# Two expert results per token kept in a lower and a higher half, read back in two steps, in a one-core Macaron block

## The chip, the core and the metric

The kernel runs on one core of a Trainium2 chip, in one launch. The metric is device time in microseconds (us). A core has these engines: PE (TensorE, matmuls, with PEld for its weight loads), DVE (VectorE), ACT (ScalarE), POOL (GpSimd) and SP (SyncE, which here only issues DMAs). Each engine runs its own instructions in the order in which they were issued, and waits on semaphores for the others. Plain DMAs are issued from SP. Indirect DMAs, which scatter or gather rows by a list of row numbers, are issued from POOL.

## The reference

Eight sequences of 512 tokens, 128 features each, pass through three residual steps:

```python
x = x + 0.5 * ffn(layernorm(x))
x = x + attention(layernorm(x))      # 16 heads of 8, causal
x = x + 0.5 * ffn(layernorm(x))      # the same weights
```

The feed-forward step is a mixture of eight experts, each 128 to 512 to 128 with a ReLU between. A router gives eight logits for a token. The two largest are taken, a softmax over the two gives the gates, and the output is the gated sum of two experts' results:

```python
topk_scores, topk_idx = jax.lax.top_k(logits, 2)
gates = jax.nn.softmax(topk_scores)
out = gates[0] * expert[topk_idx[0]](x) + gates[1] * expert[topk_idx[1]](x)
```

## The kernel before

**Groups.** Each feed-forward step handles the sequences in three groups: f0, f1, f2 for the first, g0, g1, g2 for the second, of 2, 3 and 3 sequences. For each sequence `route` (L801) computes the layernorm, the logits, the ranks and the position of each token in its expert's room. It then scatters every token twice from POOL, once for each of its two experts, to a buffer `xs` in HBM: 4 tiles of 128 tokens times 2 ranks make eight scatters for a sequence (L875). When a group's sequences are all scattered, `experts` (L924) fetches each expert's rows from `xs` into the tile `xb` with one DMA from SP (`fetch`, L933), turns them with PE (`xbT_ps`, L976), copies them into `xT` (L980), multiplies (`z`, L989), applies the ReLU into `h` (ACT at L996, DVE at L998) and multiplies again (`y`, L1013). DVE adds the bias into the tile `ysb` (L1017), and the result goes to a buffer `ys` in HBM.

**Two ways back.** For f0 to g0 each token gathers its two results by row number (`combine`, L1064; POOL gathers at L474; DVE adds at L1073). g1 and g2 are *tagged*: a scattered token carries two more numbers, its row number for rank 0 and its place in the group, so that the expert's side can work out where the token lives (`homes`, L939) and can scatter the result there directly (`send`, L956, four for each expert, L957). In the kernel before, the place is twice the token's number plus the rank, so a token's two results lie side by side. `collect` (L1099) then needs no gather: plain DMAs from SP read `ys` into a tile `yr` (L1110), DVE adds each of the two results, times its gate, to `x` (L1114), and SP writes `x` to the output (L1120). For g2, the last group, all of `collect` follows the last expert's sends: six reads, 24 adds (3 sequences, 4 tiles, 2 results) and six writes.

**Order.** The order on PE, ACT, DVE and SP is written out by hand. The program walks through units. Units 0 to 95 are one step of attention each (8 sequences, 4 head groups, 3 steps); units below 0 come before the attention, and units from 96 to 126 after it. `surround` (L1427) issues one unit: attention, a share (quota) of the current group's expert pieces, and whatever `due` names for this unit. POOL's transfers wait in two lists: `jobs` (the scatters of `route`, the gathers of `combine`) and `results` (the sends). `transfer` (L650) issues the next one of these, and jobs come first. It is called at the start and at the end of a unit, and from unit 96 on also in the middle if more than two are waiting. `transfer(second=True)` takes a job only if one of the waiting jobs is urgent, or if there are more than four and no results. `behind_mark` (L635) makes each transfer also wait for the *mark*: the ReLU, bias addition or attention mask that was issued last before it.

The eighth sequence (number 7) is routed in units 99 to 102, and its scatters are the last ones that g2's first fetch waits for:

```python
routed(u + seq + (3 if b == B - 1 else 4), *place[False][b], urgent=b in (1, 4, 5, 6, 7), ahead=b in (4, 6, 7))
...
combined(79 + 7 * i, g0, i, out)
```

The end of the kernel before is this:

```python
run(fills["g2"][0])
...
while m.results:
    m.transfer()
last = [m.collect(g2, i, out, parts=2) for i in range(3)]
step(*last)
run(*last)
```

Of the kernel before, what the change touches and what calls it, by code (L numbers as in the profile page):

```python
# [11 lines left out]
FP = mybir.dt.float32  # L12
# [436 lines left out]
class Group:  # L449


    def __init__(self, seqs, cap, key, xs, ys, tagged):
        self.seqs, self.cap, self.key, self.xs, self.ys = seqs, cap, key, xs, ys
        self.tagged, self.width = tagged, D + 2 * tagged
        self.ct = -(-cap // P)
        self.rows = cap // self.ct
        assert self.ct * self.rows == cap
        self.parts = [(t, min(3 if cap > 4 * P else 4, self.ct - t))
                      for t in range(0, self.ct, 3 if cap > 4 * P else 4)]
        self.placed = 0  # L460
        self.pieces = E * (len(self.parts) * (1 + C) + self.ct) + 1


# [19 lines left out]
class Main:  # L483
    def __init__(self, tc, ctx, aps):
# [52 lines left out]
        for e in range(4):  # L537
# [4 lines left out]
            if e == 2:  # L542
# [48 lines left out]
                       allow_small_or_imprecise_dtypes=True)  # L591

        self.place = const.tile([P, T], FP, name="place")
        nc.gpsimd.iota(self.place, [[2 * P, T]], base=0, channel_multiplier=2,
                       allow_small_or_imprecise_dtypes=True)

        self.row = {}
# [203 lines left out]
    def route(self, g, i, urgent=False, ahead=False, early=False):  # L801
# [60 lines left out]
        for r in range(2):  # L862
            nc.vector.scalar_tensor_tensor(
                sm[:, :, r, :], rank, float(r), posb, ALU.is_equal, ALU.mult
            )
        nc.vector.tensor_reduce(g.to[:, i], sm, AX.X, ALU.max)
        nc.vector.tensor_scalar(g.back[:, i], g.to[:, i], E * g.cap - 1, None, ALU.min)
        if g.tagged:
            nc.vector.tensor_copy(xn[:, :, D], g.to[:, i, :, 0])
            nc.vector.tensor_scalar(  # L870
                xn[:, :, D + 1], self.place, float(2 * N * i), None, ALU.add
            )

        def scatter(t, r):
            ins = nc.gpsimd.indirect_dma_start(  # L875
# [35 lines left out]
        nc.vector.tensor_scalar(tot, e2, 1.0, 2.0, ALU.add, ALU.mult)  # L911
        nc.vector.reciprocal(g.gates[:, i, :, 0], tot)
        nc.vector.tensor_tensor(g.gates[:, i, :, 1], g.gates[:, i, :, 0], e2, ALU.mult)
        yield

    def close_group(self, g, k):
# [7 lines left out]
    def experts(self, g):  # L924
# [14 lines left out]
        def homes(e, xb):  # L939

            row = self.row[g.cap][:rows]
            second = self.small.tile([P, CT], FP, tag="second", name=f"second_{key}_{e}")
            nc.vector.scalar_tensor_tensor(
                second[:rows, : g.ct], xb[:rows, : g.ct, D], -float(e), row,
                ALU.add, ALU.not_equal,
            )
            nc.vector.tensor_tensor(
                second[:rows, : g.ct], second[:rows, : g.ct], xb[:rows, : g.ct, D + 1], ALU.add
            )
            home[e] = self.small.tile([P, CT], I32, tag="home", bufs=7, name=f"home_{key}_{e}")  # L950
            nc.vector.scalar_tensor_tensor(
                home[e][:rows, : g.ct], row, float(2 * N * len(g.seqs) + e),
                second[:rows, : g.ct], ALU.add, ALU.min,
            )

        def send(e, t, ys):  # L956
            ins = nc.gpsimd.indirect_dma_start(  # L957
                out=g.ys[:, :],
                out_offset=bass.IndirectOffsetOnAxis(ap=home[e][:rows, t : t + 1], axis=0),
                in_=ys[:rows, t, :], in_offset=None,  # L960
            ).ins
            tc.declare_no_dep(ins, group=f"ys_{key}", reason="no two rows have the same home")
            tc.add_to_no_dep_group(f"ys_{key}", ins)
            self.in_turn(ins, scatter=True)
            self.behind_mark(ins)

# [72 lines left out]
        for e in range(E):  # L1039
            if e + 1 < E:  # L1040
                h_next, turns, wides_next = up(e + 1, loaded.pop(0))
            else:
                turns = []

            rest = downs[:1] + turns + downs[1:]
            last = turns[-1] if turns else None
            for i, piece in enumerate(wides):
                piece()
                yield
                k = -(-len(rest) // (len(wides) - i)) if rest else 0  # L1050
                for other in rest[:k]:
                    other()
                    if other is last and e + 3 < E:
                        loaded.append(fetch(e + 3))
                    yield
                rest = rest[k:]
            downs = down(e, h)
            if e + 1 < E:
                h, wides = h_next, wides_next
        for piece in downs:  # L1060
            piece()
            yield
# [36 lines left out]
    def collect(self, g, i, dst, parts=1):  # L1099

        nc = self.nc
        b = g.seqs[i]
        x = self.x[b]
        if i % 2 == 0:
            self.pair = self.p2.tile([P, 2, T, 2, D], FP, tag="ee", name=f"yr_{b}")
        yr = self.pair[:, i % 2]
        src = g.ys[2 * N * i : 2 * N * (i + 1), :].rearrange("(t p r) d -> p t r d", p=P, r=2)
        n = T // parts
        for k in range(parts):
            nc.sync.dma_start(yr[:, ts(k, n)], src[:, ts(k, n)])  # L1110
        yield
        for t in range(T):
            for r in range(2):
                nc.vector.scalar_tensor_tensor(  # L1114
                    x[:, t, :], yr[:, t, r], g.gates[:, i, t, r : r + 1], x[:, t, :],
                    ALU.mult, ALU.add,
                )
            if t % n == n - 1:
                k = t // n
                nc.sync.dma_start(  # L1120
                    dst[b].rearrange("(t p) d -> p t d", p=P)[:, ts(k, n)], x[:, ts(k, n)]
                )
            if parts == 1:
                yield
# [179 lines left out]
def macaron_kernel(  # L1304
# [51 lines left out]
    with ExitStack() as main:  # L1356
# [8 lines left out]
        g0 = m.open_group([0, 1], 351, 1, "g0")  # L1365
        g1 = m.open_group([2, 3, 4], 480, 3, "g1")
        g2 = m.open_group([5, 6, 7], 480, 4, "g2")
        order = [f0, f1, f2, g0, g1, g2]
        place = {True: {}, False: {}}
        for g in order:  # L1370
# [56 lines left out]
        def surround(n, att):  # L1427

            m.unit = n
            now = None  # L1430
            for g, fetch, start, end in plan:
                if n == fetch:
                    close(g)
                    fills[g.key] = [opened(g), g.pieces]
                if n == end:
                    run(fills[g.key][0])
                if start <= n < end:
                    now, until = fills[g.key], end
                    if g is g1 and att:
                        until = end + 7  # L1440
            quota = min(now[1], -(-now[1] // (until - n))) if now else 0
            fill = now[0] if now else iter(())
            if now:
                now[1] -= quota
            if att:
                ee = m.scores(*units[n])
            last, m.oT = m.oT, None
            if m.held is not None:
                got = m.values(*m.held)
                if got is not None:  # L1450
                    m.oT = (*m.held[:2], got)
            m.held = (*units[n], ee) if att else None
            m.evac = "dve" if att and n % seq not in (8, 9, 10) else "act"
            run(take(fill, 1 if quota else 0))
            m.evac = "act"
            if att:
                m.causal(units[n][2], ee, 0)
            m.transfer()
            if last is not None:
                m.outputs(*last)  # L1460
            if att:
                m.causal(units[n][2], ee, 1)
            if not att:
                m.additions()
            work = due.pop(n, [])
            todo = max(quota - 1, 0)
            for k, (stream, steps) in enumerate(work):
                some = todo // (len(work) - k + 1)
                run(take(stream, steps))
                run(take(fill, some))  # L1470
                todo -= some
            if n >= core and len(m.jobs) + len(m.results) > 2:
                run(take(fill, todo // 2))
                todo -= todo // 2
                m.transfer(second=True)
            run(take(fill, todo))
            m.additions()
            m.transfer(second=True)

        m.held = m.oT = None  # L1480
        with m.banks(("m", 8)):
# [32 lines left out]
                at(u + seq + 2, m.finish(b), 2, 2 if b == B - 1 else 1)  # L1514
                routed(u + seq + (3 if b == B - 1 else 4), *place[False][b], urgent=b in (1, 4, 5, 6, 7), ahead=b in (4, 6, 7))
            for i in range(2):
                combined(79 + 7 * i, g0, i, out)
            for i in range(3):
                at(tail + 2 + 3 * i, m.collect(g1, i, out), 5)
            at(tail, m.verdict(bad), 2)  # L1520
# [12 lines left out]
        with m.banks(("m", 8)):  # L1533
            for u in range(core + 2, ends):
                surround(u, False)
            run(fills["g2"][0])
            assert not due, due
            assert not m.jobs and not m.adds
            while m.results:
                m.transfer()  # L1540
            last = [m.collect(g2, i, out, parts=2) for i in range(3)]
            step(*last)
            run(*last)

    flag = nc.values_load(
        bad[0:1, 0:1], min_val=0, max_val=1,
# [50 lines left out]
```

## Time and profile before

| | |
|---|---|
| time, median of 6 runs | 715.13 us (714.58 to 716.67) |
| the profiled execution: own time | 717.68 us |
| its span, first to last instruction | 715.9 us |
| PE busy | 635.2 us (89% of the span) |
| DVE busy | 411.4 us (57%) |
| ACT busy | 340.6 us (48%) |
| POOL busy | 301.0 us (42%) |
| granted TensorE clock, mean | 0.969 |

A view of the timeline shows start, duration, engine, line, operation, output and inputs of an instruction, and in brackets how long the engine was idle before it and what ended that. Instructions that follow each other are merged (x24). The chain of waits goes back from the last instruction, at each step to what released it. SPq and POOLq are the queues' own instructions, such as the issue of a DMA. A DMA's landing is the last update of its semaphore. All times inside the trace are counted from the start of the span.

### The profile page before, as it was taken

What the parts mean: (1) busy time and instruction counts of PE and PEld (TensorE: products, weight loads), DVE (VectorE), ACT (ScalarE), POOL (GpSimd) and SP (SyncE); (2) the same over time, 40 slices, a digit from 0 to 9 for tenths busy, and PEclk for the clock granted to TensorE, in tenths of its full rate; (3) what the DMA queues carried; (4) which work ended last, traced back from release to release, by engine and by line L of the source; (5) the groups of instructions that cost most, each with busy time, mean ns of one, the idle gap of its engine ahead of it and who ended that gap; (6) DMA issues with size and microseconds to landing.
All of it is one profiled execution on the core that took longest, in us unless ns stands there. A gap on an engine that the chain in (4) does not pass through costs nothing.

```text
span 715.9 us, 13045 instructions
## 1 busy us (share of the span) xinstructions
PE 635.2 (89%) x4867; PEld 412.4 (58%) x4867; DVE 411.4 (57%) x1442; ACT 340.6 (48%) x548; POOL 301.0 (42%) x322
## 2 busy tenths in 40 slices
PE   3269989989999999999999999999999988869980
PEld 2158857756556556556656656555555556637760
DVE  6636427735466666675677677676665654233414
ACT  4034433445655665565565565556646532224420
POOL 3744627653122223314153324333244565666560
PEclk9999989999999999999999999999999998969995
DMA  8747733222409931111211110112302111235324
GB/s 263 188 132 223 181 104 97 71 59 73 97 23 152 230 113 40 29 29 35 76 33 45 44 40 30 33 39 60 71 27 73 35 37 33 74 93 136 98 56 140
DMA packets 78670, 61.06 MB, mean 85 GB/s; under 512 B 7392, under 2 KB 70792, under 8 KB 78600
## 3 DMA queue, kind: packets, MB, share of 16 engines
q1 hardware_dynamic: 69608, 42.51, 23.4%
q0 software_dynamic: 8704, 17.63, 8.6%
q8 instruction: 41, 0.67, 0.4%
q14 instruction: 29, 0.24, 0.1%
q10 hardware_dynamic: 288, 0.01, 0.0%
HBM read 26.34 MB, written 33.78 MB: 84 GB/s over the span
## 4 chain that ended last, share of the span: by engine, by line
PE 81%; DVE 5%; DMA 2%; another core or an unknown queue 2%; ACT 2%; issue 1%; POOL 1%; POOLq 0%; ACTq 0%; DVEq 0%
PE st L1201 13%; PE o L1227 11%; PE y_f L1013 11%; PE z_g L989 11%; PE z_f L989 10%; PE y_g L1013 10%; PE qkv_ps_a L1139 3%; PE kT_ps L1178 2%; PE qT_ps L1178 2%; PE otok_ps L1245 2%; PE xbT_ps_f L976 2%; PE xbT_ps_g L976 1%; DVE x L1114 1%; PE proj_ps L1266 1%
## 5 line engine op out<-in xcount | busy, mean ns | idle before, releaser
L1208 ACT ACTIVATE ee<-st 128x768 f32<-128x768 f32 (+1 forms) x192 | 159.0, 881 | 109.6 <-PE st L1201 91.8
L474 POOL DMA_INDIRECT yt_f<-ys,back_f x64 | 64.9, 1014 | 136.7 <-DVE ee L1215 56.0
L1215 DVE TENSOR_TENSOR ee<-ee,keep 128x256 f32<-128x256 f32 (+1 forms) x192 | 93.7, 508 | 26.1 <-ACT ee L1208 26.0
L1013 PEld LDWEIGHTS y_g<-w_sb,h_g 128*120 128x120 f32 (+1 forms) x704 | 87.3, 184 | 27.9 <-issue 22.4
L875 POOL DMA_INDIRECT xs<-xn_g,to_g x64 | 64.0, 1001 | 92.8 <-DVE ee L1215 36.1
L1013 PEld LDWEIGHTS y_f<-w_sb,h_f 128*120 128x120 f32 (+1 forms) x704 | 85.8, 182 | 28.5 <-issue 17.3
L989 PE MATMUL z_g<-xT_g,w_sb 128*128 128x480 f32 (+1 forms) x192 | 94.5, 580 | 8.4 <-ACT xT_g L980 6.0
L1201 PE MATMUL st<-qT,kT 32*128 32x512 f32 (+3 forms) x1024 | 96.1, 467 | 4.0 <-ACT kT L1184 1.7
L1013 PE MATMUL y_f<-w_sb,h_f 128*120 128x128 f32 (+1 forms) x704 | 93.9, 277 | 0.2 <-DVE h_f L998 0.2
L1013 PE MATMUL y_g<-w_sb,h_g 128*120 128x128 f32 (+1 forms) x704 | 93.0, 277 | 0.6 <-DVE o_tok L1250 0.3
L989 PE MATMUL z_f<-xT_f,w_sb 128*128 128x480 f32 (+1 forms) x192 | 91.8, 568 | 1.0 <-ACT xT_f L980 1.0
L1227 PE MATMUL o<-ee,vpad 128*32 128x512 f32 (+3 forms) x1024 | 89.4, 442 | 0.8 <-DVE ee L1215 0.8
L996 ACT ACTIVATE h_f<-z_f,b1T 128x480 f32<-128x480 f32 (+1 forms) x86 | 53.5, 623 | 73.5 <-PE z_f L989 55.9
L957 POOL DMA_INDIRECT ys<-ysb_g,home_g x64 | 64.0, 1000 | 45.6 <-issue 12.1
L1017 DVE TENSOR_TENSOR ysb_f<-y_f,b_sb 120x128 f32<-120x128 f32 (+1 forms) x88 | 25.1, 288 | 82.9 <-PE y_f L1013 65.8
L1017 DVE TENSOR_TENSOR ysb_g<-y_g,b_sb 120x128 f32<-120x128 f32 (+1 forms) x88 | 25.3, 288 | 76.3 <-PE y_g L1013 52.2
L996 ACT ACTIVATE h_g<-z_g,b1T 128x480 f32<-128x480 f32 (+1 forms) x71 | 45.7, 646 | 48.9 <-PE z_g L989 37.9
L1201 PEld LDWEIGHTS st<-qT,kT 32*128 32x128 f32 x1024 | 43.1, 183 | 34.3 <-issue 8.8
L875 POOL DMA_INDIRECT xs<-xn_n,to_f x40 | 39.0, 974 | 37.3 <-issue 8.8
L1227 PEld LDWEIGHTS o<-ee,vpad 128*32 128x32 f32 x1024 | 23.5, 108 | 52.4 <-issue 8.6
L989 PEld LDWEIGHTS z_g<-xT_g,w_sb 128*128 128x128 f32 x192 | 30.7, 198 | 34.7 <-issue 19.7
L989 PEld LDWEIGHTS z_f<-xT_f,w_sb 128*128 128x128 f32 x192 | 31.5, 201 | 14.9 <-issue 9.5
(186 smaller groups left out, 780.8 us busy)
## 6 DMA issues: line engine op xcount, KB each, us to landing
w_sb<-in_L_ffn_W_dram SPq DMA_DIRECT2D x16, 256.0 KB
xs<-zeros SPq DMA_DIRECT2D x8, 487.5 KB
xb_g<-xs SPq DMA_DIRECT2D x16, 243.8 KB
xb_f<-xs SPq DMA_DIRECT2D x16, 240.0 KB
ys<-ysb_f SPq DMA_DIRECT2D x16, 240.0 KB
ys<-zeros SPq DMA_DIRECT2D x2, 1536.0 KB
x<-in_L_attn_x_dram SPq DMA_DIRECT2D x8, 256.0 KB
xs<-zeros SPq DMA_DIRECT2D x1, 1920.0 KB
```

What stands on the lines that cost most here:

```text
L474: ins = op(*args, **kw)
L875: ins = nc.gpsimd.indirect_dma_start(out=g.xs[:, :], out_offset=bass.IndirectOffsetOnAxis(ap=g.to[:, i, t, r : r + 1], axis=0), in_=xn[:, ...
L957: ins = nc.gpsimd.indirect_dma_start(out=g.ys[:, :], out_offset=bass.IndirectOffsetOnAxis(ap=home[e][:rows, t : t + 1], axis=0), in_=ys[:r ...
L989: nc.tensor.matmul(z[:, :n], self.w1_sb[:, e, ts(c, P)], xT[:, n0 : n0 + n], start=True, stop=True,)
L996: ins = nc.scalar.activation(dst, z[:, :n], AF.Relu, bias=bias)
L1013: nc.tensor.matmul(y[:rows], h[:, c, ts(t, rows)], self.w2_sb[:, e, c, :], start=(c == 0), stop=(c == C - 1),)
L1017: ins = nc.vector.tensor_tensor(ys[:rows, t, :], y[:rows], self.b2_sb[:rows, e], ALU.add)
L1178: self.nc.tensor.transpose(tp[:, ts(t, P)], pad[:, t, 4 * g : 4 * g + 4, :].rearrange("p h s -> p (h s)"), self.ident,)
L1201: nc.tensor.matmul(st[:, h, c0 : c0 + N - kt * P], kT[r0 : r0 + SLOT, ts(kt, P)], qT[r0 : r0 + SLOT, kt * P :], start=True, stop=True,)
L1208: nc.scalar.activation(ee[:, two, :width], st[:, two, :width], AF.Exp)
L1215: ins = self.nc.vector.tensor_tensor(d, d, self.keep.unsqueeze(1).unsqueeze(1).to_broadcast([P, 2, len(parts), P]), ALU.min,)
L1227: self.nc.tensor.matmul(self.o[h * SLOT : (h + 1) * SLOT, kt * P :], self.vpads[b % 2][:, kt, 4 * g + h, :], ee[:, h, c0 : c0 + n], start= ...
```

## The change

**Results in two halves.** The first half of `ys` takes, for every token of the group, the result of the one of its two experts that has the lower number, and the second half that of the other one. To tell which is which, `route` compares the expert numbers of the two ranks (`which`, `swap`), puts the lower expert's row number into the tag (`apart`), and swaps the two gates where needed. `homes` now adds N times the number of sequences where a row is not the lower one's. `collect` reads each half with a DMA of its own, [128 x 4 x 128], where a read before took both results, [128 x 4 x 256] for g1 and two of [128 x 2 x 256] for each sequence of g2.

**g2's collect in two steps.** The last expert, number 7, is never the lower of two. The three `collect` streams of g2 are created at the start (`g2.ends`). When the pieces of expert 6 and the upward multiplications of expert 7 have been issued, `experts` first issues all waiting sends and then the reads of the three lower halves. After that come the downward multiplications of expert 7 with its sends, the reads of the higher halves, the 12 adds of the lower results, and the 12 adds of the higher ones with the six writes. A group named "lower" takes out the dependency between the early reads and expert 7's sends.

**Eight scatters in one row.** From unit 98 on two more transfers are issued in the middle of a unit if more than one job is waiting. The eight scatters of sequence 7 are then issued in two units (4 and 4), where they took three (2, 3 and 3).

**Gathers of g0's second sequence** are entered at unit 84, where it was 86.

```diff
-        nc.gpsimd.iota(self.place, [[2 * P, T]], base=0, channel_multiplier=2,
+        nc.gpsimd.iota(self.place, [[P, T]], base=0, channel_multiplier=1,
...
         nc.vector.tensor_reduce(g.to[:, i], sm, AX.X, ALU.max)
+        if g.tagged:
+            which = small.tile([P, T, 2], I32, tag="which", name=f"which_{key}")
+            nc.vector.tensor_scalar(which, g.to[:, i], E - 1, None, ALU.bitwise_and)
+            swap = small.tile([P, T], FP, tag="swap", name=f"swap_{key}")
+            nc.vector.tensor_tensor(swap, which[:, :, 0], which[:, :, 1], ALU.is_gt)
+            apart = small.tile([P, T], FP, tag="apart", name=f"apart_{key}")
+            nc.vector.tensor_tensor(apart, g.to[:, i, :, 1], g.to[:, i, :, 0], ALU.subtract)
+            nc.vector.tensor_tensor(apart, apart, swap, ALU.mult)
+            nc.vector.tensor_tensor(xn[:, :, D], apart, g.to[:, i, :, 0], ALU.add)
+            nc.vector.tensor_scalar(xn[:, :, D + 1], self.place, float(N * i), None, ALU.add)
         nc.vector.tensor_scalar(g.back[:, i], g.to[:, i], E * g.cap - 1, None, ALU.min)
-        if g.tagged:
-            nc.vector.tensor_copy(xn[:, :, D], g.to[:, i, :, 0])
-            nc.vector.tensor_scalar(
-                xn[:, :, D + 1], self.place, float(2 * N * i), None, ALU.add
-            )
...
         nc.vector.tensor_tensor(g.gates[:, i, :, 1], g.gates[:, i, :, 0], e2, ALU.mult)
+        if g.tagged:
+            lo, hi = g.gates[:, i, :, 0], g.gates[:, i, :, 1]
+            nc.vector.tensor_tensor(tot, hi, lo, ALU.subtract)
+            nc.vector.tensor_tensor(tot, tot, swap, ALU.mult)
+            nc.vector.tensor_tensor(lo, lo, tot, ALU.add)
+            nc.vector.tensor_tensor(hi, hi, tot, ALU.subtract)
...
-            nc.vector.tensor_tensor(
-                second[:rows, : g.ct], second[:rows, : g.ct], xb[:rows, : g.ct, D + 1], ALU.add
+            nc.vector.scalar_tensor_tensor(
+                second[:rows, : g.ct], second[:rows, : g.ct], float(N * len(g.seqs)),
+                xb[:rows, : g.ct, D + 1], ALU.mult, ALU.add,
             )
...
+            if e == E - 1 and g.ends:
+                tc.declare_no_dep(ins, group="lower", reason="the last expert is none's lower")
...
             downs = down(e, h)
             if e + 1 < E:
                 h, wides = h_next, wides_next
+        if g.ends:
+
+            while self.results:
+                self.transfer()
+            for collect in g.ends:
+                next(collect)
         for piece in downs:
...
-        src = g.ys[2 * N * i : 2 * N * (i + 1), :].rearrange("(t p r) d -> p t r d", p=P, r=2)
         n = T // parts
-        for k in range(parts):
-            nc.sync.dma_start(yr[:, ts(k, n)], src[:, ts(k, n)])
-        yield
-        for t in range(T):
-            for r in range(2):
-                nc.vector.scalar_tensor_tensor(
-                    x[:, t, :], yr[:, t, r], g.gates[:, i, t, r : r + 1], x[:, t, :],
-                    ALU.mult, ALU.add,
-                )
+        src = g.ys[: 2 * N * len(g.seqs), :].rearrange(
+            "(r b t p) d -> r b p t d", r=2, b=len(g.seqs), p=P
+        )
...
+        ins = nc.sync.dma_start(yr[:, 0], src[0, i])
+        if g.ends:
+            self.tc.add_to_no_dep_group("lower", ins.ins)
+            yield
+        nc.sync.dma_start(yr[:, 1], src[1, i])
+        yield
+        if g.ends:
+            for t in range(T):
+                add(t, 0)
+            yield
+        for t in range(T):
+            if not g.ends:
+                add(t, 0)
+            add(t, 1)
...
                 m.transfer(second=True)
+                if n >= core + 2 and len(m.jobs) > 1:
+                    m.transfer(second=True)
+                    m.transfer(second=True)
...
-                combined(79 + 7 * i, g0, i, out)
+                combined(79 + 5 * i, g0, i, out)
...
-            last = [m.collect(g2, i, out, parts=2) for i in range(3)]
-            step(*last)
-            run(*last)
+            step(*g2.ends)
+            step(*g2.ends)
+            run(*g2.ends)
```

More of the change, by code (lines that the diff above doesn't have):

```diff
@@ L459, in __init__ @@
                       for t in range(0, self.ct, 3 if cap > 4 * P else 4)]
-        self.placed = 0
+        self.placed, self.ends = 0, ()
         self.pieces = E * (len(self.parts) * (1 + C) + self.ct) + 1
@@ L1104, in collect, with add @@
         if i % 2 == 0:
-            self.pair = self.p2.tile([P, 2, T, 2, D], FP, tag="ee", name=f"yr_{b}")
+            self.pair = self.p2.tile([P, 2, 2, T, D], FP, tag="ee", name=f"yr_{b}")
         yr = self.pair[:, i % 2]
-        src = g.ys[2 * N * i : 2 * N * (i + 1), :].rearrange("(t p r) d -> p t r d", p=P, r=2)
         n = T // parts
-        for k in range(parts):
-            nc.sync.dma_start(yr[:, ts(k, n)], src[:, ts(k, n)])
+        src = g.ys[: 2 * N * len(g.seqs), :].rearrange(
+            "(r b t p) d -> r b p t d", r=2, b=len(g.seqs), p=P
+        )
+        def add(t, r):
+            nc.vector.scalar_tensor_tensor(
+                x[:, t, :], yr[:, r, t], g.gates[:, i, t, r : r + 1], x[:, t, :],
+                ALU.mult, ALU.add,
+            )
+        ins = nc.sync.dma_start(yr[:, 0], src[0, i])
[3 more added lines that the diff above has]
+        nc.sync.dma_start(yr[:, 1], src[1, i])
         yield
+        if g.ends:
+            for t in range(T):
+                add(t, 0)
+            yield
         for t in range(T):
-            for r in range(2):
-                nc.vector.scalar_tensor_tensor(
-                    x[:, t, :], yr[:, t, r], g.gates[:, i, t, r : r + 1], x[:, t, :],
-                    ALU.mult, ALU.add,
-                )
+            if not g.ends:
+                add(t, 0)
+            add(t, 1)
             if t % n == n - 1:
@@ L1367, in macaron_kernel @@
         g2 = m.open_group([5, 6, 7], 480, 4, "g2")
+        g2.ends = [m.collect(g2, i, out, parts=2) for i in range(3)]
         order = [f0, f1, f2, g0, g1, g2]
```

## The prediction

> **What bounds the kernel now.** I read the page's busy line first, then its forty slices, because the share of an engine is an average over stages with different limits.
>
> ```profile
> PE 635.2 (89%) x4867; PEld 412.4 (58%) x4867; DVE 411.4 (57%) x1442; ACT 340.6 (48%) x548; POOL 301.0 (42%) x322
> PE   3269989989999999999999999999999988869980
> ```
>
> PE carries the span but for three places: the start, a dip near slice 36, and the last slices. The change touches the second and the third. Next, the busy time by windows (columns: window, length, then busy of PE, PEld, DVE, ACT, POOL, granted clock, DMA share, GB/s), and who PE waits for in the attention stage (us in total, times, longest).
>
> ```profile
> 240.00:590.00 350.00, 341.62 (x2933) 205.38 (x2932) 234.76 (x758) 200.19 (x318) 126.77 (x125) 1.00 0.20 54
> 624.00:634.00 10.00, 1.03 (x4) 0.69 (x4) 0.69 (x4) 0.38 (x1) 5.92 (x6) 0.64 0.62 144
> PE qkv_ps_a L1139 <- DVE o_tok L1250: 1.7, 5, 0.7
> PE o L1227 <- DVE ee L1215: 0.8, 1, 0.8
> ```
>
> In attention PE is busy 341.6 of 350 us; DVE has 115 us to spare, and all PE waits on it add up to 3.2 us. From 624 to 634 PE does almost nothing. The POOL timeline there (start, length, idle time before and its releaser) shows the row of scatters of sequence 7 that g2's first fetch waits for:
>
> ```profile
> 611.48 0.99 POOL L875 DMA_INDIRECT xs<-xn_g,to_g  x1 [1.69 <-DVE ex_g L907]
> 612.77 0.98 POOL L875 DMA_INDIRECT xs<-xn_g,to_g  x1 [0.30 <-issue]
> 615.08 0.96 POOL L875 DMA_INDIRECT xs<-xn_g,to_g  x1 [1.33 <-issue]
> ...
> 621.43 0.97 POOL L875 DMA_INDIRECT xs<-xn_g,to_g  x1 [0.30 <-issue]
> ```
>
> The last lands 2.2 us later, SP issues the fetches at 623.79, the first lands at 627.04. Then the waits of 615 to 640 show something else:
>
> ```profile
> ACT xT_g L980 <- remote: 14.5, 1, 14.5
> ```
>
> ACT takes PE's first transpose only at 633.62, 6 us after it was done by PE's records, so g2's start need not follow the row. What the profile cannot name ("remote") I do not count on.
>
> Last, the chain of waits and the timeline of the tail:
>
> ```profile
> 697.77 2.73 DMA ys<-ysb_g,home_g
> 700.51 0.02 issue
> 700.52 3.01 DMA yr<-ys
> 703.53 0.03 issue
> 703.56 0.36 DVE x L1114
> ...
> 703.56 7.89 DVE L1114 SCALAR_TENSOR_TENSOR x<-yr,gates_g,x 128x128 f32<-128x128 f32 x24 [7.70 <-DMA yr<-ys]
> 704.97 6.87 SPq L1120 DMA_DIRECT2D out_dram<-x  x6
> ```
>
> PE ended at 694.6. The last send leaves at 697.77 and lands 2.73 later; six reads follow, the first landing after 3.01; 24 adds run back to back for 7.89 us; the last write is issued at 711.47 and lands at 713.51. Every one of these is on the path. The sends are paced by POOL, 1.29 us apart, and DVE waited 7.70 us ahead of its adds.
>
> The profiled execution took 717.68 us (span 715.9, and 1.8 around it), 2.55 above the median of 715.13. I work out differences in it and apply them to the median.
>
> **Part 1, the lower half read early: −3.94 us, of which part is given back.** By the order of instructions in the changed kernel, the three lower reads wait for the last send of expert 6, and the three upper reads for the last of expert 7; both stand on SP's queue in that order, with nothing else behind them that is needed earlier. Expert 6's last send was issued at 692.52 and landed at 695.66. So the lower reads leave at about 695.7, the first lands 3.0 us later at 698.7, and the twelve lower adds (12 × 0.329 = 3.95 us) end at about 702.7 if their data keep up, which is ahead of the first upper landing at 703.5. Twelve adds remain behind it: 12 × 0.329 = 3.95 in place of 7.89. The upper reads are three of 256 KB; the six of before landed at 703.53, 704.23, 705.74, 706.40, 707.74 and 708.48, so three come about 1.0 apart, under the 1.31 us that four adds of a sequence take. DVE stays the bound, and the last write goes out 3.94 us sooner. Two writes come per 1.3 us instead of per 2.6; each moves 128 KB, and the writes of before were spread over 6.5 us with the last landing 2.0 after its issue; I add nothing for that and 0.3 in the range. Removed reads cost nothing: total bytes are equal. A read row is now 512 B where two results of a token stood together as 1024 B. In the trace a 1024 B packet takes 54.8 ns on its engine, one of 520 B 34 to 38 and one of 512 B 27 to 31, so half the row is about half the time; at worst (38 against 27.4) the upper reads take 1.4 times their part, 1.4 us per sequence and 0.2 behind the adds, put at 0.5 in the bound.
>
> **What the early reads cost: +0.7 us, from 0 to +2.0.** They run beside expert 7's last scatters. The trace has no read beside a send at the tail, but it has the fetches of g2 (four of 244 KB, issued 623.79 to 625.72) beside g1's sends: those issued at 624.00, 625.30, 626.60 and 627.89 landed 4.70, 4.82, 4.10 and 2.82 us later, and one alone takes 2.73. The last scatter at 697.77 comes 2.1 us after the first early read, as the send at 625.30 to 626.60 does after the fetches; that says +1.4 to +2.1, of which I take 2.0 as the end. But the early reads are three, not four, in fewer bytes (768 KB against 975 KB), and the read queue should be nearly empty (six reads took 8 us, so three take some 5: to 700.5), as for the send at 627.89, which lost 0.1. I take a value between, nearer the later row: +0.7. This is the least certain term of the sum.
>
> [...]
>
> **Part 2, sequence 7's scatters in one row: +0.1 us, from −0.41 to +0.62.** Their transfers move up on the list only, and the order of POOL's instructions is that of before. What changes is the time. On DVE, four more small operations (`which`, `swap`, `apart` twice) stand ahead of the copy of a y piece that the first scatter also waits for (610.91 to 611.20, then +0.28). Small dependent operations follow one another by 0.21 us in the rows of the routing, independent ones by 0.08: 3 × 0.21 + 0.08 = 0.71 us, of which DVE had 0.1 idle. So the first scatter goes at about 612.1, +0.62. Against it stands the gap of 1.33 ahead of the third scatter, where 0.30 is usual and nothing named is waited for: if it is gone in the new order of issue, 1.03 comes back, −0.41 in all. PE's start of g2 need not follow, by the 6 us above. I take +0.1.
>
> **Part 3, DVE's added work in attention: +0.2 us, from 0 to 7.2.** Each tagged sequence gets the 0.71 above and four operations on the gates, another 0.71; five of the six sequences fall beside attention: 5 × 1.43 = 7.2 us on DVE. Its cover is the 115 us in which DVE is idle in that window. The waits of PE on DVE are 3.2 us for 234.8 us of DVE work; in that proportion 7.2 more gives 0.1, and since a routing chain comes in one piece I take 0.2. If the cover were gone, all 7.2 would be PE's.
>
> **What costs nothing.** The first gathers of the second sequence of g0 come two units sooner in the list, but POOL's order does not change by it. Collecting g1 takes six reads instead of three: three more issues of about 0.47 us on SP, whose queue there holds the fetches of `xb` with four buffers, asked for a unit ahead. `homes` has one operation in place of one. If that cover failed, a read ahead of a fetch would cost its 0.47.
>
> **Sum:** −3.94 + 0.7 + 0.1 + 0.2 = −2.94, so 715.13 − 2.94 = 712.2 us.
>
> **The rivals.**
>
> *The row pays and the reads collide with nothing.* −3.94 + 0 − 0.41 = −4.35, so 710.8. For it: the 0.1 of the send at 627.89, and an unexplained gap that may be of one execution. Against it: the three sends before that.
>
> *The early reads hold up expert 7's sends.* The last scatter lands at +2.0 and the upper reads, short rows, lag +0.5; −3.94 + 2.5 + 0.3 (parts 2 and 3) = −1.14, so 714.0: nearly no change. For it: 4.70 and 4.82 against 2.73.
>
> *DVE becomes the bound (the slower side).* A routing chain is serial on DVE between `ee` products (L1215, 508 ns each, 192 of them) that PE's `o` waits for. If every added 1.43 us pushes those products back and PE's buffers are empty by then, PE loses 7.2 us in attention: −2.94 − 0.2 + 7.2 = +4.1, 719.2. It decides from about 3.1 + 1.4 = 4.5 us carried over, 63% of the 7.2. For it: `o <- ee` with 0.8 in one piece. Against it: only 3.2 us of waits of this kind in 350.
>
> *It does not do what it says.* If the lower reads, on one queue with others or for a dependence of the whole buffer `ys`, land only with the upper, all 24 adds stay behind: 0 + 0.1 + 0.2, about 715.4. The order of instructions speaks against it.
>
> **How the numbers follow.** The forecast gets 0.64, with its own range of 711.0 to 713.6 (part 1's collision from 0 to +2.0, the others about their values). The row that pays gets 0.12, the hold-up 0.14, DVE as the bound 0.06, no early read 0.04. The range over all leaves out DVE's case, and the outer ends of those on both sides: 710.4 to 714.8. What a measurement of this kernel can tell from no change is about 0.2%, 1.43 us: below 713.70 is faster, above 716.56 slower. Faster holds the forecast and the row that pays: 0.76. Same holds the hold-up and no early read: 0.18. Slower holds DVE's case: 0.06.
>
> **What would show it.** In the changed profile's tail: three reads issued at about 695.7 less or plus the shift of the stages before, three at about 700.5 to 702; the twelve lower adds done before the first upper read lands; a run of twelve adds of 3.95 us behind it; the last send's landing at 2.7 (no hold-up) to 4.7 us (full hold-up) after its issue. In the middle: the first scatter of sequence 7 at about 612.1, the last at 621.0 to 622.1, and whether ACT's first `xT_g` follows it. In attention: PE busy again about 341 of 350 with PE's waits on DVE near 3 us. I am wrong if PE's waits on DVE grow by over 4 us, if the last lower add ends after the upper reads have landed, or if g2's first matmul moves by over a microsecond.

## The result, and the profile after

The changed kernel takes 722.40 us (median of 17 runs, 717.22 to 725.70) against 715.91 for the kernel before over 38 runs: ratio 1.0082 [1.0063, 1.0102], 6.5 us slower. The profiled execution took 718.07 us (span 716.3), the low end of its runs; its granted clock did not drop around 94 us, where the profile of before has 6.8 us at 0.5. So the two profiles are compared stage by stage.

The busy line and the PE slices of the changed kernel:

```profile
PE 631.6 (88%) x4867; PEld 410.4 (57%) x4867; DVE 416.9 (58%) x1490; ACT 340.0 (47%) x548; POOL 301.5 (42%) x322
PE   3279989999999999999999999989999978649990
```

DVE has 48 more instructions; the dip near slice 36 has grown deeper. The windows and PE's waits in attention:

```profile
240.00:590.00 350.00, 339.85 (x2922) 204.26 (x2919) 236.96 (x790) 200.14 (x315) 127.97 (x125) 1.00 0.18 51
624.00:634.00 10.00, 1.03 (x4) 0.69 (x4) 4.07 (x12) 0.00 (x0) 7.56 (x9) 0.50 0.54 129
PE qkv_ps_a L1173 <- DVE o_tok L1284: 1.7, 5, 0.7
PE o L1261 <- DVE ee L1249: 0.8, 1, 0.8
```

PE's named waits on DVE are those of before. From 624 to 634 POOL is busy 7.56 us, where it was 5.92. Its timeline from sequence 7's scatters on (POOL), ACT's wait from 615 to 640, and PE's first transposes of g2 with the ACT copy that takes them:

```profile
609.57 0.99 POOL L880 DMA_INDIRECT xs<-xn_g,to_g  x1 [1.90 <-DVE ex_g L912]
...
613.11 0.97 POOL L880 DMA_INDIRECT xs<-xn_g,to_g  x1 [1.25 <-issue]
...
619.47 0.97 POOL L880 DMA_INDIRECT xs<-xn_g,to_g  x1 [0.30 <-issue]
...
628.53 0.99 POOL L969 DMA_INDIRECT ys<-ysb_g,home_g  x1 [0.30 <-issue]
629.82 0.99 POOL L969 DMA_INDIRECT ys<-ysb_g,home_g  x1 [0.30 <-issue]
631.12 1.09 POOL L969 DMA_INDIRECT ys<-ysb_g,home_g  x1 [0.30 <-DMA ys<-ysb_g,home_g]
...
637.67 0.99 POOL L969 DMA_INDIRECT ys<-ysb_g,home_g  x1 [0.30 <-issue]
642.81 0.99 POOL L969 DMA_INDIRECT ys<-ysb_g,home_g  x1 [4.15 <-ACT h_g L1010]
ACT xT_g L994 <- remote: 19.9, 1, 19.9
625.33 1.03 PE L990 MATMUL xbT_ps_g<-ident,xb_g 120*128 120x120 f32 x4 [5.52 <-DMA xb_g<-xs]
635.76 0.56 ACT L994 COPY xT_g<-xbT_ps_g 128x480 f32<-128x480 f32 x1 [19.91 <-remote]
```

From the third scatter on, POOL goes from one indirect DMA to the next with gaps of 0.30 us until 638.7. In the kernel before it paused twice in this stretch:

```profile
631.31 0.98 POOL L957 DMA_INDIRECT ys<-ysb_g,home_g  x1 [1.15 <-issue]
634.16 0.99 POOL L957 DMA_INDIRECT ys<-ysb_g,home_g  x1 [1.87 <-DVE second_g L947]
```

PE's first transposes of g2 start at 625.33 and end, by PE's records, at 626.37, but their semaphore comes at 635.74, 9.4 us later, and ACT's `xT_g` only then (635.76). Before, it was 5.4 us. The ends in PE's records are modelled, so the trace does not tell whether the multiplication itself or only its semaphore is late; "completion" below means the semaphore. g2's first `z` multiplication starts at 636.37, where it was 634.24. The tail (SP, then DVE):

```profile
698.61 1.47 SPq L1138 DMA_DIRECT2D yr<-ys  x3
705.34 1.46 SPq L1142 DMA_DIRECT2D yr<-ys  x3
703.55 3.25 DVE L1133 SCALAR_TENSOR_TENSOR x<-yr,gates_g,x 128x128 f32<-128x128 f32 x12 [4.93 <-DMA yr<-ys]
708.07 3.41 DVE L1133 SCALAR_TENSOR_TENSOR x<-yr,gates_g,x 128x128 f32<-128x128 f32 x12 [1.27 <-DMA yr<-ys]
```

The early reads are early, twelve adds are done before the upper half lands, and twelve remain. But the last send, issued at 700.22, lands 5.1 us later, where it was 2.7.

### The profile page after: what moved, and what is told of

The parts are those of the page before. It is cut to its first block, busy times and chain, and to the rows that moved or that the text cites. A ratio compares the mean times of both kernels' runs of the same rounds, so it can differ in the third digit from the quotient of the medians.

```text
span 716.3 us, 13103 instructions
## 1 busy us (share of the span) xinstructions
PE 631.6 (88%) x4867; PEld 410.4 (57%) x4867; DVE 416.9 (58%) x1490; ACT 340.0 (47%) x548; POOL 301.5 (42%) x322
## 5 line engine op out<-in xcount | busy, mean ns | idle before, releaser
L1003 PE MATMUL z_f<-xT_f,w_sb 128*128 128x480 f32 (+1 forms) x192 | 88.9, 551 | 1.0 <-ACT xT_f L994 1.0
```

Source lines behind the costliest of these rows:

```text
L1003: nc.tensor.matmul(z[:, :n], self.w1_sb[:, e, ts(c, P)], xT[:, n0 : n0 + n], start=True, stop=True,)
```

## The experiments

The sessions on the chip were of two kinds: in some PE's completions stall ahead of g2, and the kernel before takes 713 to 716 us; in others they do not, and it takes 702 to 703. The measurement above is of the first kind. What decides it is not known (one chip number gave both), so the text says sessions where the expectations say chips. The stall ahead of g2 is not all that a stalling session costs: e16 below, which has none there, takes 713.6 us, where the row alone takes 702.0 and 702.3 in quiet sessions. By the profiles some 7 of these 11 us lie ahead of attention (first `st` at 150.4 against 143.2 and 143.9); no run here tells why. Ratios are to the kernel before in the same session; "late" is the time from PE's first `xbT` of g2 to ACT's first `xT_g`, 1.07 us at the least.

| run | kernel | session | ratio [95%] | late, us |
|---|---|---|---|---|
| e1_row | row alone | quiet | 0.9993 [0.9978, 1.0007] | 1.07 |
| e2_norow | changed without row | quiet | 0.9969 [0.9952, 0.9986] | 1.07 |
| e3_late | changed, all reads late | quiet | 0.9983 [0.9968, 0.9999] | 1.07 |
| e4_rank_late | the same, halves by rank | quiet | 0.9987 [0.9970, 1.0003] | 1.07 |
| e5_changed | changed | quiet | 0.9970 [0.9955, 0.9986] | 1.07 |
| e6_changed | changed | quiet | 0.9978 [0.9962, 0.9995] | 1.07 |
| e7_row | row alone | quiet | 0.9989 [0.9973, 1.0006] | 1.07 |
| e8_norow | changed without row | quiet | 0.9984 [0.9970, 0.9998] | 1.07 |
| e9_before | before | stalling | 712.93 us, one run | 6.4 |
| e10_changed | changed | stalling | 723.46 us, one run | 12.7 |
| e11_flood | before, four more DMAs | stalling | 712.92 us, one run | 5.3 |
| e12_flood_changed | changed, four more DMAs | stalling | 729.12 us, one run | 15.2 |
| e13_row | row alone | stalling | 1.0099 [1.0069, 1.0130] | 14.7 |
| e14_pace | changed, sends' old pace | stalling | 1.0028 [1.0005, 1.0051] | 7.7 |
| e15_hold | changed, sends held | stalling | 0.9968 [0.9943, 0.9992] | 1.07 |
| e16_row_hold | row, sends held | stalling | 0.9964 [0.9943, 0.9985] | 1.07 |
| e17_hold | changed, sends held | stalling | 0.9951 [0.9932, 0.9969] | 1.07 |
| e18_changed | changed | stalling | 1.0086 [1.0062, 1.0109] | 9.8 |

### One part at a time

The gathers' edit was not run alone. In e2_norow, which has it, POOL's instructions stand in the order of before, and g0's gathers leave at the same times after the first `st` as in e1_row, to 0.7 us. The row alone, and the changed kernel without it, differ by these lines:

```diff
                 m.transfer(second=True)
+                if n >= core + 2 and len(m.jobs) > 1:
+                    m.transfer(second=True)
+                    m.transfer(second=True)
```

> The kernel before with only the two extra transfers per unit, so that sequence 7's eight scatters are issued in two units and not three. On every engine the instructions stand in the order of before; only the marks that POOL's transfers wait for move, and with them g1's sends, which may go some 3 transfers sooner. Theory A (the row and the freer sends run into g2's first fetches and hold up PE's start on g2): most of what the changed kernel lost, +4 to +6 us against before. Theory B (the added DVE operations ahead of the scatters start them later, and PE's start on g2 follows by more than that): nothing of it is here, -0.5 to +0.6 us. Theory C (the tail loses what it was to gain): 0 here too.

> The changed kernel without the two extra transfers per unit: halves, early lower reads and all added DVE operations stay. Theory A: the loss is gone and the tail's gain shows, -2.5 to -1 us against before. Theory B: still slower by +4 to +6.5 us. Theory C: as the changed kernel, +5 to +6.5 us, with the last send landing some 5 us after its issue.

For e3_late the early reads go behind all sends:

```diff
             while self.results:
                 self.transfer()
-            for collect in g.ends:
-                next(collect)
...
-            self.tc.add_to_no_dep_group("lower", ins.ins)
...
-            if e == E - 1 and g.ends:
-                tc.declare_no_dep(ins, group="lower", reason="the last expert is none's lower")
...
+            step(*g2.ends)
             step(*g2.ends)
             step(*g2.ends)
```

> The changed kernel with all six reads of g2 behind the last send of expert 7 (the halves, the added DVE operations and the row stay). The profile of the changed kernel has the last landing held up by 2.4 us and the rest of the tail 4.1 us shorter, so without the early reads the last send should land 2.7 us after its issue and 24 adds should stand behind the reads. Theories A and B: slower than the changed kernel by about 1.7 us, +7 to +9 against before. Theory C: faster than the changed kernel by 2 us or more, +2 to +5 against before.

For e4_rank_late a token's halves are its ranks, which needs no `swap`:

```diff
-            which = small.tile([P, T, 2], I32, tag="which", name=f"which_{key}")
...
-            nc.vector.tensor_tensor(xn[:, :, D], apart, g.to[:, i, :, 0], ALU.add)
+            nc.vector.tensor_copy(xn[:, :, D], g.to[:, i, :, 0])
...
-            lo, hi = g.gates[:, i, :, 0], g.gates[:, i, :, 1]
...
-            nc.vector.tensor_tensor(hi, hi, tot, ALU.subtract)
```

> As the kernel with late reads, and the halves by rank and not by expert, which needs none of the eight added DVE operations per sequence (the result is the same); the row stays. Theory A: as the kernel with late reads, +6 to +9 us against before. Theory B: the loss is gone, -0.5 to +1 us. Theory C: 0 to +1 us.

None of the four was slower than before, so none of theories A to C held as put. In each, ACT's wait names its releaser (waits of e1_row, 605 to 625):

```profile
ACT xT_g L980 <- PE xbT_ps_g L976: 9.3, 1, 9.3
```

The kernel before took 702.5 us here, which called for the changed kernel itself in such a session.

> The changed kernel as it is, once more. In the profiles that the prediction is compared with, PE's semaphore for the first transpose of g2 came 5.4 us after PE's record ended in the kernel before and 9.4 us after in the changed one; in the four runs so far it came 0 to 0.1 us after, and none of those kernels was slower than before. Theory D (what the changed kernel lost is a longer stall of PE's completions in the gap ahead of g2, which only some chips show): where the stall is absent, -2.5 to -0.5 us against before; where it is there, +4 to +7. Theory A or B (the order of the work costs it everywhere): +4 to +7 on either.

> The changed kernel again, for a chip on which PE's completions stall ahead of g2 (the first transpose of g2 done over 2 us after PE's record ends). Theory D: if the stall is there, slower than before by 4 to 7 us, with ACT's first xT_g over 8 us behind PE's xbT; if not, faster by 1 to 3 us, with xT_g 1.1 us behind it. Theory A or B: slower on any chip; the run before this one (faster by 2.2 us) speaks against them.

> The kernel before with only the row. If the stall is there and grows with the sends that run unbroken through the gap: +3 to +5 us; if it does not depend on them: within 1 us. Without the stall: within 0.7 us of before, as on the first chip tried.

> The changed kernel without the row. If the stall is there and grows with the unbroken sends: -2 to 0 us against before, as their pace is that of before; if it grows with what else the change adds: +3 to +6. Without the stall: -2.5 to -1 us, as on the first chip tried.

The changed kernel is faster there, by 2.2 and 1.4 us. That is what theory D expected without a stall; the runs with only the row or all but the row could not yet say which part lengthens the stall, and the changed kernel without the row met no stalling session.

### A session that stalls

One profile of each kernel, and one of each with four more plain DMAs of 1024 rows of 256 B, meant to crowd the DMA engines:

```diff
         loaded = [fetch(0), fetch(1)]
+        if key == "g2":
+            for k in range(4):
+                nc.sync.dma_start(
+                    self.xs[0][1024 * k : 1024 * (k + 1), :64],
+                    self.aps["x"].rearrange("b n d -> (b n) d")[1024 * k : 1024 * (k + 1), :64],
+                )
```

> The kernel before, for a profile on the same chip as the next three. Without the stall (theory D): ACT's first xT_g of g2 1.1 us behind PE's first xbT (it was 6.5 behind it in the profile that the prediction read), the last send landing 2.4 to 4.2 us after its issue, the end 17.9 to 19.6 us behind the last send. The first scatter of sequence 7 about 0.6 us sooner after the end of attention than in the changed kernel.

> The changed kernel beside it. From the prediction's sum, stage by stage against the run before this: attention 0 to +1 us, the row's first scatter +0.6, xT_g 1.1 us behind xbT, the last send landing later by 0.7 to 2, the end 3 us nearer to the last send; in all -3 to -1 us.

> The kernel before with four more DMAs on SP behind g2's second fetch: each copies 1024 rows of 256 B from an input to a buffer in HBM that nothing reads any more, to crowd the DMA engines in the gap ahead of g2. If crowded DMAs alone hold up PE's completions: ACT's first xT_g comes 3 us or more behind PE's first xbT, where 1.1 is undisturbed, and the end is later by at least as much. If not: 1.1 us still, and only the third and fourth fetches (and with them PE's later pieces) are late, by 5 to 10 us.

> The same four DMAs in the changed kernel. If crowding holds up PE and the unbroken sends add to it: xT_g behind xbT by more than in the run before this, by 2 us or more. If crowding does not hold up PE: 1.1 us, and the difference between the two flooded kernels is that between the two plain ones, -3 to -1 us.

The stall was back, and e9 and e10 missed: 6.4 and 12.7 us in place of 1.1, and the changed kernel slower by 10.5 us. The four DMAs did not lengthen it in the kernel before (5.3 against 6.4); in the changed one it went from 12.7 to 15.2, one run each. The moment at which the late completions come follows POOL. In e9, POOL's sends stopped at 627.6 and PE's last three completions came between 624.8 and 629.9; in e11 they stopped at 627.9, and the completions came by 630.3; in the changed kernel's profiles POOL did not stop, and each of the last two completions came 6 to 11 us after the one before it.

Why POOL goes on there is in the marks. Each send waits for the youngest matmul result (`h` or `ysb`) issued before it. With the row, two more transfers leave the list in each of two units, so every send of g1 behind them waits for the mark that the send four places ahead of it had before. In the kernel before, the seventh send behind the row waits for `ysb_g1_7_2` and the eighth for `ysb_g1_7_3`, the very pieces that hang; with the row it is the eleventh and the twelfth. Kernels that make the transfers behind the row skip as many turns (`debt`) test that. With 2 per unit of the row (e14_pace) all sends get their old marks back; with 4 (e15_hold) they wait for marks four places later still:

```diff
+        self.debt = 0
...
+        if self.debt and not self.jobs:
+            self.debt -= 1
+            return
...
                 if n >= core + 2 and len(m.jobs) > 1:
                     m.transfer(second=True)
                     m.transfer(second=True)
+                    m.debt += 2
```

> The kernel before with only the row, for a chip that stalls PE. Theory E (on such a chip PE's last completions before it runs dry wait until POOL's unbroken chain of indirect DMAs stops; the row moves the marks of g1's sends three places sooner, so POOL stops some 10 us later): with the stall, POOL's chain runs on through the gap, xT_g over 9 us behind xbT, +4 to +9 us against before. If the row is not the cause, 6.5 us behind as before, within 1 us of before. Without the stall: within 0.7 us of before, xT_g 1.1 us behind xbT.

> The changed kernel with its row, early reads and added DVE operations, where the units after the row skip as many transfers as the row moved ahead: all sends of g1 and g2 wait for the marks that they had before. Theory E: with the stall, POOL pauses in the gap as before, xT_g 5 to 7 us behind xbT, and the tail's gain shows: -3 to 0 us against before. If the DVE operations or the early reads bring the loss on: +4 to +9 us as the changed kernel. Without the stall: -2.5 to -1 us.

> The same with four skipped transfers per unit of the row: g1's first sends behind the row wait for PE's last pieces of g1, and seven more for g2's first hidden tiles. Theory E: with the stall, POOL's chain stops at the row's end, xT_g 1 to 3 us behind xbT, -7 to -3 us against before. If POOL has no part in it: as the run before this. Without the stall: -2.5 to +0.5 us (sends later by up to 10 us, which POOL has room for until the tail).

The row alone costs 7.5 us. POOL and ACT in its profile:

```profile
630.77 0.98 POOL L957 DMA_INDIRECT ys<-ysb_g,home_g  x1 [0.30 <-issue]
632.06 0.98 POOL L957 DMA_INDIRECT ys<-ysb_g,home_g  x1 [0.31 <-issue]
634.07 0.98 POOL L957 DMA_INDIRECT ys<-ysb_g,home_g  x1 [1.03 <-issue]
638.42 0.56 ACT L980 COPY xT_g<-xbT_ps_g 128x480 f32<-128x480 f32 x1 [23.42 <-remote]
```

Its `xbT` stood at 623.73, so `xT_g` is 14.7 us behind. With the sends held, POOL's chain ends early (e15_hold, POOL, ACT and DVE):

```profile
624.88 0.99 POOL L973 DMA_INDIRECT ys<-ysb_g,home_g  x1 [0.30 <-issue]
626.48 0.99 POOL L973 DMA_INDIRECT ys<-ysb_g,home_g  x1 [0.60 <-issue]
629.39 0.99 POOL L973 DMA_INDIRECT ys<-ysb_g,home_g  x1 [1.93 <-DVE second_g L962]
629.23 0.56 ACT L998 COPY xT_g<-xbT_ps_g 128x480 f32<-128x480 f32 x1 [10.39 <-PE xbT_ps_g L994]
628.80 0.29 DVE L1035 TENSOR_TENSOR ysb_g<-y_g,b_sb 120x128 f32<-120x128 f32 x1 [2.62 <-remote]
```

`xbT` was at 628.16: 1.07 us, as without a stall. The stall is not gone altogether: the last `ysb` of g1 comes 6.0 us after the end of PE's record (1.3 us after POOL went quiet at 627.47). But it is over before g2's transposes end. e14_pace missed its -3 to 0: with the sends' old marks most of the loss is gone, and 1.9 us (0.4 to 3.6 by its interval) remain. The next section says where they lie.

> The kernel before with the row and with the held sends, without the early reads and the added DVE operations: only the marks of POOL's transfers differ from before. With the stall, theory E: xT_g 1 to 3 us behind xbT, and as the stall of before goes too, -6 to -2 us against before, where the row alone was +7.5. If the held sends helped only together with the early reads: +3 to +8. Without the stall: -1 to +1 us.

> The changed kernel with the held sends once more, beside the two others. With the stall: -4 to -1 us against before (measured -2.3 before). Without it: -3 to +0.5 us, as the changed kernel there or a little behind it, if sends that come later cost nothing at the tail.

> The changed kernel beside them. With the stall: +5 to +9 us, POOL unbroken through the gap and xT_g over 9 us behind xbT. Without: -2.5 to -1 us, xT_g 1.1 us behind.

Held sends turn the changed kernel's +5.9 us into -3.0 in one session; there the row with held sends stands at -2.65, where the row alone had +7.5 in e13's session. e18 and e17 ran in one session and differ only in the marks of the sends. e15/e17 is the version that beats both kernels where PE stalls; in a quiet session it was not run. What its early reads and halves add to the held sends is not shown: -3.0 and -2.65 differ by less than their intervals.

## Why the prediction was wrong, point by point

The terms of the sum, from the profiles. "Stalling" is the mean of three profiles of the changed kernel (the measured one, e10, e18) less that of the kernels with before's tail and operations: five for attention, scatter and tail (before, e9, e11, e13, e16), and the three with before's sends for the stall. "Quiet" is e5 and e6 less the row alone (e1, e7).

| term | predicted | stalling | quiet |
|---|---|---|---|
| attention, first `st` to end of last `proj` | +0.2 | 444.8 - 442.7 = +2.2 | 440.0 - 440.0 = 0.0 |
| `to_g` to the row's first scatter | +0.62 | 2.44 - 1.71 = +0.7 | 2.35 - 1.75 = +0.6 |
| the row to `xbT` | -1.03 to 0 | -0.1 | -0.2 |
| `xbT` to `xT_g` | 0 | 11.0 - 6.1 = +4.9 | 0.0 |
| last send to the end | -3.94 + 0.7 = -3.2 | 15.6 - 17.8 = -2.1 | 16.1 - 18.8 = -2.7 |

With +0.4 between attention and `to_g` and +0.5 from `xT_g` to the last send (against the three with before's sends) the stalling column makes +6.5, where +6.5 and +5.9 were measured. The agreement is partly luck: the stretch ahead of attention, which the change hardly touches, is not in the table. It was 1.5 us shorter in these three profiles than in the five, and it varies from 146.2 to 152.2 us among stalling profiles.

**Part 2 is the step that failed.** I wrote that "the order of POOL's instructions is that of before" and that only the time changes, and I followed the marks of the eight scatters. The marks of the sends behind them move as well, and I priced none of them. What the runs showed in place of that zero is the sends running on through the gap and `xT_g` 4.9 us later behind `xbT` in stalling sessions (0.0 in quiet ones). I wrote that I do not count on "remote" in ACT's wait, and yet took the 6 us behind it as slack ("PE's start of g2 need not follow"). The profile of before held both halves:

```profile
629.17 0.99 POOL L957 DMA_INDIRECT ys<-ysb_g,home_g  x1 [0.30 <-issue]
630.72 0.29 DVE L1017 TENSOR_TENSOR ysb_g<-y_g,b_sb 120x128 f32<-120x128 f32 x1 [6.72 <-remote]
633.57 0.29 DVE L1017 TENSOR_TENSOR ysb_g<-y_g,b_sb 120x128 f32<-120x128 f32 x1 [2.56 <-remote]
633.62 0.56 ACT L980 COPY xT_g<-xbT_ps_g 128x480 f32<-128x480 f32 x1 [14.53 <-remote]
```

There are POOL's two pauses inside the gap, and `ysb` at 630.72, 0.6 us after POOL went quiet at 630.16, and `ysb` and `xT_g` at 633.57 and 633.62, 1.3 us after it went quiet at 632.29. One of my signs of being wrong came: g2's first matmul moved by over a microsecond. A wait of 14.5 us with no named releaser on the path was a term with a sign that I could not know, and belonged in the range. The rest of part 2 came as worked out: the four operations cost 0.6 to 0.7 us, and the 1.03 us gap ahead of the third scatter did not go.

**Part 3, DVE in attention: +0.2 predicted, 0.0 in quiet sessions, +2.2 where PE stalls.** The waits named by the profile were right (PE's on DVE did not grow), and nothing of the rival that DVE becomes the bound shows in quiet sessions. Six profiles with the added operations in stalling sessions read 444.1 to 445.2 us there (e12, at a mean granted clock of 0.961 where the six have 0.969 to 0.974, 446.0), all five without them 442.2 to 443.2. This is inside my bound of 7.2 and above the value I took. Most of it sits at the very end: from PE's last `aT_ps` to `proj_ps` it is 1.39 us in all five profiles without the operations, and 2.0 to 3.4 in the six with them. In the measured profile (ACT, then DVE):

```profile
589.10 0.59 ACT L1296 COPY aT<-aT_ps 128x512 f32<-128x512 f32 x1 [1.92 <-PE y_g L1027]
589.95 0.29 DVE L1031 TENSOR_TENSOR ysb_g<-y_g,b_sb 120x128 f32<-120x128 f32 x1 [3.50 <-remote]
```

PE's record of `aT_ps` ends at 586.92, 2.2 us ahead of ACT's copy. So this looks like a second, shorter stall of PE's completions and not like DVE's work; that is read from the profiles, and no run tests it, nor which edit brings it on (the gathers' edit lies in attention too). For e14 the sum is +2.0 in attention, +0.6 at the row, +1.7 in the stall (7.7 against 6.1) and -2.4 at the tail: in all +1.9, as measured, with the other stages of its one profile left out.

**Part 1 was right, with two sizes off.** The lower reads left at 698.61, ahead of the last send, and the lower adds were done 1.3 us before the upper half. Adds over different tiles overlap (records of 0.35 us start 0.26 apart): twelve took 3.41 us, 0.28 each, where pairs on one tile took 0.33. So the adds gave -4.5 us, not -3.94. Against that, the early reads held up the last send by 2.4 us in the measured profile (5.13 against 2.75), above the bound of 2.0 and far above the 0.7 that I took; by 1.2 to 2.7 in six profiles with them in stalling sessions (mean 4.33 against 2.47). It is not theirs alone: in one quiet profile without early reads (e7) the last send also took 4.2 us. The rows of g2's fetches beside sends (1.4 to 2.1 us) were nearer to it than what I took, and I should have taken their end.

**The rivals.** None is what happened. The hold-up of the last send came, and left the tail 2.1 us ahead all the same. The slower side that I priced, DVE as the bound, was not the slower side that came. In quiet sessions, where the stall is absent, the kernel gained 2.2 and 1.4 us against the 2.94 predicted, mostly from the tail.

## What to carry to other kernels

When an edit moves transfers on a queue, list for every later instruction of that queue what it waited for before and after: an unchanged order can hide that a chain which used to pause now runs on. A long wait on the path whose releaser the profile cannot name is a term of unknown size and sign; look what each other engine does at the moment it ends, and put it in the range. Measure an edit in more than one session before trusting the sign of a change under one per cent: this one measured +0.8% in one kind of session and -0.2 to -0.3% in the other.

## What the runs showed of the hardware

In stalling sessions, the completions of PE's last pieces before it runs dry come late while POOL issues indirect DMAs with gaps of 0.30 us: 6 to 11 us apart with POOL at 1.29 us a piece (changed), and the last ones 0.6 to 2.4 us after POOL pauses (before, e9, e11). With the sends held, the last piece of g1 is still 4 to 6 us late (e15 to e17), and g2's first transposes are not (`xT_g` 1.07 us behind `xbT`). That POOL's chain makes the difference there is shown by e17 against e18, of one session, which differ only in the sends' marks: 1.07 and 9.8 us. e16 against e13 says the same from two sessions (1.07 and 14.7).

POOL's chain is not enough by itself: in e1, a quiet session, its sends go on with gaps of 0.30 us from 613.0 to 620.8, and PE's pieces of that stretch are taken 0.04 us after their records end. How the one holds up the other is not shown, nor whether it is POOL's issuing or the writes of its DMAs, which move together in every run. Four extra plain DMAs of 1024 small rows did not lengthen the stall in the kernel before (5.3 against 6.4 us); in the changed one they may have (15.2 against 12.7, one run each).

The profiles of stalling sessions lack records: 6,966 to 7,294 semaphore updates where those of quiet sessions have 9,782 to 9,888, for the same programs. No run here shows whether the missing records and the late completions have one cause, or whether taking the profile is itself what makes a session stall.
